# A graph network on one core: no scratch writes between the gathers, attention fetched two chunks ahead, products copied out by ScalarE

## The chip, the cores and the metric

The kernel runs on one core of a Trainium2 chip. The metric is the device time of one execution in microseconds (us). Five engines work side by side, each through its own queue of instructions: TensorE (PE; its weight loads are listed as PEld), VectorE (DVE), ScalarE (ACT), GpSimd (POOL) and SyncE (SP, which here only issues transfers). SBUF is the on-chip memory of 128 partitions, PSUM the small memory that TensorE writes its products to.

## The reference, cut to what matters

There are 6250 nodes with 128 features and 200,000 edges, sorted by destination `dst`; `src` is random. Two convolutions over edges are followed by one attention over edges. All is float32.

```python
def mesh_conv(x, src, dst, ea, w1, b1, g, bt, w2, b2):
    m = jnp.concatenate([x[dst], x[src], ea], axis=-1) @ w1 + b1
    m = jax.nn.silu(group_norm(m, g, bt))
    m = m @ w2 + b2
    out = jax.ops.segment_sum(m, dst, num_segments=n)
    return out / jnp.clip(cnt, 1.0)[:, None]

h = mesh_conv(x, ...);  h = silu(group_norm(h));  h = h + time_embedding
h = mesh_conv(h, ...);  h = silu(group_norm(h)) + x
q, k, v = (h @ w + b).reshape(n, 8, 16)            # three products
logits = (q[dst] * k[src]).sum(-1) * scale + (edge_attr @ ew + eb)
amax = segment_max(logits, dst)
pe = jnp.exp(logits - amax[dst])
w = pe / jnp.clip(segment_sum(pe, dst)[dst], 1e-06)
o = segment_sum(w[:, :, None] * v[src], dst).reshape(n, D) @ ow + ob
return h + group_norm(o, an_g, an_b)
```

What matters for the change: rows of a table are fetched for every edge by `src` (a gather), rows for `dst` come from a product with a one-hot matrix, and the two are added (convolutions) or multiplied (attention).

## The kernel before

**Stages.** After a preparation there are three edge stages in a row: `conv(1)`, `conv(2)` and attention (`pipeline(3, Stage(bp))`, L1374). Each goes over 196 chunks of 1024 edges (8 tiles of 128). A stage ends with node work for the nodes that are left (`last_nodes`); most nodes are done in batches of four times 128 while the edges run (`conv_nodes`, `attention_nodes`, advanced one piece per step of the pipeline).

**Fetching a chunk** (`fetch` of each `Stage`). `loads` (L598) has SP bring the `pk` rows (the window of 112 destination rows, one of three buffers) and, for every two chunks, `ohT`: the destinations of 2048 edges spread over 112 partitions (896 KB, L592) and their attributes (L595). `gather` (L620) has POOL issue eight indirect transfers (L622), one for each tile of 128 edges, from `b_d` (convolutions, 512 bytes a row) or `kv_d` (attention, keys and values, 1024 bytes a row) into a tile `g`. After the eight it issues `rest` writes of zeros to a scratch tile `nst2` (L634), which nobody reads. `issue_after` keeps their place in POOL's queue: behind the gathers of this chunk and ahead of the next. `REST` (L28) gives 1, 2 and 4 such writes a chunk for the three stages.

**Working on a chunk.** `compared` (L613) has ACT turn `ohT` into a one-hot matrix in two passes (L615, L616). `products` has PE multiply it with `pk` (L1002 in the convolutions, L1181 in attention, there into three PSUM tiles `qe` of at most three tiles of edges each, 136 columns a tile: 128 of q and 8 of the edges' bias). In the convolutions `first` adds the gathered rows (L1008). In attention `first` calls `logits` (L1185): VectorE multiplies `qe` with the gathered keys, once for each `qe` tile (L1190), ACT copies the bias columns to `ebs` (L1191), VectorE sums over each head (L1193) and adds the bias (L1195).

**Attention, later work.** Chunks are taken together in runs of up to eight. `maxima` is a generator that finds the running maxima of a run: transposes on PE, scans on VectorE (L1222, L1225), a subtraction (L1233), the exponent on ACT (L1235) and eight small products (L1237). `second` advances it between the instructions of the chunk that it works on: a one-hot (L639), `add_late` (L1273 to L1279), `weighted` (ACT copies into `v` at L1246, VectorE's product with the gathered values at L1247), the sums by destination on PE (L1254), and `merge_late` (L1287 to L1269). Chunk n-9 is worked on in step n. The pool `gp` holds 11 tiles `g`, `vp` one tile `v`.

**Order.** `pipeline` (L713) writes out the order by hand: a step n fetches chunk n + `ahead`, and so on down the list. `in_order` (L701) then fixes that order on VectorE, SP, ACT and PE, each for itself; POOL is not in that list. With `ahead = 2` (convolutions) the products of chunk n+1 come right after the fetch, with `ahead = 1` (attention) at the end of the step. Waits between engines are added from what the tiles need: a tile in a pool of n buffers waits until the last reader of the n-th tile before it is done.

The heart of the step, and the end of `maxima`'s use in `second`:

```python
        stage.root(run)
        if n + ahead < NCH:
            compared(ks[n + ahead])
        stage.second(run, [ks.pop(c) for c in seconds])
        if n < NCH:
            stage.first(ks[n])
```

Of the kernel before, what the change touches and what calls it, by code (L numbers as in the profile page):

```python
# [8 lines left out]
FP = mybir.dt.float32  # L9
BF = mybir.dt.bfloat16  # L10
I32 = mybir.dt.int32
AF = mybir.ActivationFunctionType
ALU = mybir.AluOpType
AX = mybir.AxisListType
# [7 lines left out]
P = 128  # L22
D = 128
H = 8
HD = 16
NT = 8
CH = NT * P
REST = {1: 1, 2: 2, 3: 4}  # L28
G = 8
GC = 2  # L30
BN = 4
# [4 lines left out]
DB = D + H  # L36
# [9 lines left out]
def kernel(ctx: ExitStack, tc: tile.TileContext, x, src, dst, eat, w, out):  # L46
# [9 lines left out]
    nc = tc.nc  # L56
    N = x.shape[0]
    EW = src.shape[1]
    NCH = EW // NT
# [5 lines left out]
    const = ctx.enter_context(tc.tile_pool(name="const", bufs=1))  # L65
# [7 lines left out]
    hpc = gpc.enter_context(tc.tile_pool(name="hpc", bufs=1))  # L73
# [5 lines left out]

    ident = const.tile([P, P], FP, name="ident")  # L80
    make_identity(nc, ident)
    iota_i = const.tile([P, P], I32, name="iota_i")
    nc.gpsimd.iota(iota_i, pattern=[[1, P]], base=0, channel_multiplier=0)
    iota_pi = const.tile([P, 1], I32, name="iota_pi")
    nc.gpsimd.iota(iota_pi, pattern=[[1, 1]], base=0, channel_multiplier=1)
# [234 lines left out]
    for t in pk:  # L320
        nc.vector.memset(t, 0.0)

    temb = const.tile([P, D], FP, name="temb")
    squares = {n: const.tile([P, D], FP, name=f"w_{n}") for n in ("c1_w2", "c2_w2", "ow")}
    qkv_t = const.tile([P, 3, D], FP, name="qkv_t")

# [386 lines left out]
    def pipeline(i, stage, aside=iter(())):  # L713

        start = len(nc.cur_bb.bb.instructions)  # L720
        ends, todo = steps_of(i)
        starts = {n: j for j, (n, _) in enumerate(plans[i])}
        ahead = stage.ahead
        ks, under_way = {}, []
        for c in range(ahead):
            ks[c] = stage.fetch(c)
            compared(ks[c])
        stage.products(ks[0])
        for n, seconds in enumerate(todo):
            if n + ahead < NCH:  # L730
                ks[n + ahead] = stage.fetch(n + ahead)
            if n + 1 < NCH and ahead == 2:
                stage.products(ks[n + 1])
            run = [ks[c] for c in ends.get(n, ())]
            stage.root(run)
            if n + ahead < NCH:
                compared(ks[n + ahead])
            stage.second(run, [ks.pop(c) for c in seconds])
            if n < NCH:
                stage.first(ks[n])  # L740
            if n + 1 < len(todo) and todo[n + 1]:
                stage.early(ks[todo[n + 1][0]])
            if n in starts:
                for _ in aside:
                    pass
                under_way.append(stage.batch(starts[n]))
            for g in list(under_way):
                if next(g, STOP) is STOP:
                    under_way.remove(g)
            if n > 4:  # L750
                next(aside, None)
            if n < NCH:
                stage.reduce(ks[n])
            if n + 1 < NCH and ahead == 1:
                stage.products(ks[n + 1])
        stage.flush()
        for g in (*under_way, aside):
            for _ in g:
                pass
        in_order(start)  # L760
# [205 lines left out]
    def conv(i):  # L966
# [4 lines left out]
        with ExitStack() as es:  # L971
            pool = lambda n, b, **kw: es.enter_context(tc.tile_pool(name=f"{n}{i}", bufs=b, **kw))
# [72 lines left out]
            class Stage:  # L1045
# [4 lines left out]
                def fetch(self, c):  # L1050
# [3 lines left out]
                    k.h = hs[c % len(hs)]  # L1054
                    return k

                def products(self, k):
                    hidden(k, [(k.ohT[:KW], k.pk[:KW, :D])])

# [103 lines left out]
    with ExitStack() as es:  # L1163
        pool = lambda n, b, **kw: es.enter_context(tc.tile_pool(name=f"{n}a", bufs=b, **kw))
        pools = {"oh": pool("oh", 2), "ps": pool("ps", 1, space=PSUM)}
        gp, wk, vp = pool("gp", G + 3), pool("wk", 2), pool("vp", 1)
        ps_ = pools["ps"]
        iota = ps_.tile([P, D], FP, name="iota")
        nc.vector.tensor_copy(iota, iota_j)
# [3 lines left out]

        def products(k, terms):

            for a in range(0, NT, TB):
                qe = ps_.tile([P, TB, DB], FP, name="qe", tag="qe", bufs=3)
                for t in range(min(TB, NT - a)):
                    e = slice((a + t) * P, (a + t + 1) * P)
                    for j, (lhs, rhs) in enumerate(terms):  # L1180
                        nc.tensor.matmul(qe[:, t, :], lhsT=lhs[:, e], rhs=rhs,  # L1181
                                         start=(j == 0), stop=(j == len(terms) - 1))
                k.qe.append(qe)

        def logits(k, lg):  # L1185
            ebs = wk.tile([P, NT, H], FP, name="ebs")
            for a, qe in zip(range(0, NT, TB), k.qe):
                n = min(TB, NT - a)
                kk = k.g[:, a:a + n, :D]
                nc.vector.tensor_tensor(kk, qe[:, :n, :D], kk, ALU.mult)  # L1190
                nc.scalar.copy(ebs[:, a:a + n, :], qe[:, :n, D:])  # L1191
            l3 = wk.tile([P, NT, H], FP, name="l3")
            nc.vector.tensor_reduce(  # L1193
                l3, k.g[:, :, :D].rearrange("p t (h c) -> p t h c", c=HD), AX.X, ALU.add)
            nc.vector.tensor_tensor(lg, l3, ebs, ALU.add)  # L1195

        def load_runs(run, bp):

# [97 lines left out]
            add(k, t3[:, bass.ds(k.win, 2), :], 2)  # L1296

        class Stage:
            ahead = 1
            sums, late, nb = [], [], None  # L1300
            lg, j = None, 0

# [5 lines left out]
            def fetch(self, c):  # L1308
                k = loads(c, pools, a_d[3], self.ahead)
                k.g = gp.tile([P, NT, KV], FP, name="g")  # L1310
                gather(k, k.g, kv_d, REST[3])
                k.qe = []
                return k

            def products(self, k):
                products(k, [(k.ohT[:KW], k.pk[:KW])])

            def first(self, k):
                if self.j == 0:
# [14 lines left out]
            def second(self, run, ks):  # L1334


                pieces = iter(())
                if run:
                    pieces = maxima(run, self.lg, self.nb, self.bp)
                    self.nb, self.j = None, 0  # L1340
                for n, k in enumerate(ks):
                    mine = pieces if n == len(ks) - 1 else iter(())
                    next(mine, None)
                    onehot(k, pools, iota)
                    next(mine, None)


                    if self.late:
                        add_late(self.late.pop(0))
                    next(mine, None)  # L1350
                    weighted(k)
                    nc.scalar.copy(k.v[:, :, VK:VK + H], k.wl)
                    nc.scalar.copy(k.v[:, :, VK + H], ef[:, k.c * NT:(k.c + 1) * NT])
                    sums(k, VK + H + 1)
                    if self.sums:
                        merge_late(self.sums[0])
                        self.late.append(self.sums.pop())
                    self.sums.append(k)
                for _ in pieces:
                    pass  # L1360

            def batch(self, j):
# [17 lines left out]
        def left(k):  # L1380
            lp = pools["left"]
            left_rows(k, pools, a_d[3], "qe", [P, TB, DB], 3)
            k.g = gp.tile([P, NT, KV], FP, name="g")
            gather(k, k.g, kv_d)
            k.qe = []
            products(k, [(k.ohf.rearrange("p t e -> p (t e)"), k.rows), (k.ea, webl)])
            lg = lp.tile([P, NT, H], FP, name="l_lg")
            logits(k, lg)
            neg = lp.tile([P, 4, P], FP, name="l_neg")
            part = lp.tile([P, H, 2], FP, name="l_part")  # L1390
            junk = lp.tile([P, 4, P], FP, name="l_junk")
            for a in range(2):
                nc.vector.tensor_scalar(neg, k.ohf[:, 4 * a:4 * a + 4, :], 1.0, BIG, ALU.subtract, ALU.mult)
                for h in range(H):
                    bc = ps_.tile([P, 4, P], FP, name="l_bc", tag="blk")
                    for t in range(4):
                        nc.tensor.transpose(bc[:, t, :], lg[:, 4 * a + t, h:h + 1].to_broadcast([P, P]), ident)
                    nc.vector.tensor_tensor_reduce(
                        junk, bc, neg, 1.0, -BIG, ALU.add, ALU.max, part[:, h, a:a + 1])
            cm = lp.tile([P, H], FP, name="l_cm")  # L1400
            nc.vector.tensor_reduce(cm, part, AX.X, ALU.max)
            me = ps_.tile([P, NT, H], FP, name="l_me", tag="pe")
            for t in range(NT):
                nc.tensor.matmul(me[:, t, :], lhsT=k.ohf[:, t, :], rhs=cm, start=True, stop=True)
            nc.vector.tensor_tensor(lg, lg, me, ALU.subtract)

            nc.vector.tensor_scalar(lg, lg, 0.0, None, ALU.min)
            k.pe = lp.tile([P, NT, H], FP, name="l_pe")
            nc.scalar.activation(k.pe, lg, AF.Exp)
            weighted(k)  # L1410
            sums(k, VK)
            tt = t3[:, bass.ds(k.win, 1), :]
            merge(k, M[:, bass.ds(k.win, 1), :], None, cm[:, None, :], 1)
            add(k, tt, 1)
# [43 lines left out]
```

## Time and profile before

| | |
|---|---|
| time, median of 3 runs | 6840.58 us (6835.94 to 6841.69) |
| the profiled execution | 6827.89 us |
| span of its profile, first to last instruction | 6826.1 us |
| busy PE / DVE / ACT / POOL | 3811.6 (56%) / 5134.4 (75%) / 3310.5 (48%) / 5154.2 (76%) us |
| granted clock of TensorE, mean | 0.736 |
| gathers, L622 | 4704, mean 959 ns (convolutions) and 980 ns (attention) |
| scratch writes, L634 | 1372, mean 432 ns, 593.2 us busy |
| transfers | 800.41 MB, mean 117 GB/s |

How to read it: a line of a group names the line of the kernel, engine, operation, output and inputs (sizes as partitions x elements), the count, then the busy time and the mean duration of one in ns, then the engine's idle time just before them and what ended it. In a view by time the first two numbers are the start and the duration in us. A wait is put down to the event that came last. Matmul times are modelled, and POOL's spans are rough.

### The profile page before, as it was taken

How to read it: one execution, taken by the hardware profiler on the slowest of the kernel's cores; microseconds unless marked ns; L12 is line 12 of the kernel's file. 1: busy time of each engine (PE TensorE's matmuls, PEld its weight loads, DVE VectorE, ACT ScalarE, POOL GpSimd, SP SyncE). 2: the span in 40 equal slices, each digit the busy share in tenths (PEclk: the TensorE clock that was granted, in tenths of full speed). 3: DMA queues.
4: the chain of work that ended last, by engine and by line, in shares of the span. 5: the costliest groups of instructions: out<-in, count | busy, mean ns of one | idle time of the engine just before them, and what ended most of it. 6: DMA issues, size and time to landing. Idle time of an engine off the chain costs nothing. (4 is left out here: it accounts for less than half of the span.)

```text
span 6826.1 us, 73476 instructions
## 1 busy us (share of the span) xinstructions
PE 3811.6 (56%) x20957; PEld 3602.1 (53%) x20958; DVE 5134.4 (75%) x7564; ACT 3310.5 (48%) x5293; POOL 5154.2 (76%) x6090
## 2 busy tenths in 40 slices
PE   5555555555554555555555555455555555555555
PEld 4555555555554555555555555445545555555554
DVE  7877888888886777777777777556677777777777
ACT  5666566666665555555555555322233333333332
POOL 5777777777775777777777777577777777777774
PEclk8777777777777767677777777677777777777777
DMA  5544444444443433334444344354555555555543
GB/s 155 127 109 103 101 118 107 113 109 108 108 112 82 99 98 96 96 98 104 111 104 109 104 108 110 100 136 134 136 142 138 143 143 143 138 141 144 143 135 84
DMA packets 414317, 800.41 MB, mean 117 GB/s; under 512 B 101813, under 2 KB 274984, under 8 KB 379496
## 3 DMA queue, kind: packets, MB, share of 16 engines
q0 software_dynamic: 175616, 411.34, 24.3%
q1 hardware_dynamic: 232646, 380.69, 19.9%
q10 hardware_dynamic: 5632, 3.51, 0.2%
q8 instruction: 172, 2.82, 0.2%
q14 instruction: 251, 2.06, 0.1%
HBM read 754.19 MB, written 40.96 MB: 116 GB/s over the span
## 5 line engine op out<-in xcount | busy, mean ns | idle before, releaser
L622 POOL DMA_INDIRECT g<-b_d,src_i x3136 | 3006.1, 959 | 951.9 <-issue 913.6
L1032 PE MATMUL u<-h,oh 128*128 128x129 f32 (+1 forms) x6272 | 1276.9, 386 | 1474.2 <-ACT h L1027 1473.9
L1032 PEld LDWEIGHTS u<-h,oh 128*128 128x128 f32 x6272 | 1178.6, 289 | 1557.0 <-ACT h L1027 1553.3
L622 POOL DMA_INDIRECT g<-kv_d,src_i x1568 | 1536.8, 980 | 500.8 <-issue 470.4
L1002 PE MATMUL m<-pk,ohT 117*128 117x128 f32 x6272 | 1005.3, 328 | 340.9 <-DVE h L1008 298.2
L1254 PE MATMUL u<-v,oh 128*128 128x145 f32 x3136 | 760.1, 430 | 764.7 <-DVE nm L1287 763.0
L1002 PEld LDWEIGHTS m<-pk,ohT 117*128 117x128 f32 x6272 | 965.9, 243 | 368.9 <-DVE h L1008 320.1
L1254 PEld LDWEIGHTS u<-v,oh 128*128 128x128 f32 x3136 | 707.0, 312 | 799.7 <-issue 799.7
L1008 DVE TENSOR_TENSOR h<-m,g 128x1024 f32<-128x1024 f32 x392 | 478.7, 1221 | 817.8 <-DMA g<-b_d,src_i 800.9
L1010 ACT ACTIVATE sq<-h 128x1024 f32<-128x1024 f32 x392 | 414.3, 1057 | 817.6 <-DVE h L1008 817.0
L1027 ACT ACTIVATE h<-h 128x1024 f32<-128x1024 f32 x392 | 414.3, 1057 | 653.8 <-DVE h L1026 637.2
L1190 DVE TENSOR_TENSOR g<-qe,g 128x384 f32<-128x384 f32 (+1 forms) x588 | 294.6, 511 | 549.0 <-DMA g<-kv_d,src_i 512.0
L615 ACT ACTIVATE ohT<-ohT,minus_p 112x1024 f32<-112x1024 f32 x588 | 670.5, 1140 | 16.4 <-DMA ohT<-rel_d 16.2
L616 ACT ACTIVATE ohT<-ohT 112x1024 f32<-112x1024 f32 x588 | 621.5, 1057 | 18.6
L634 POOL MEMSET nst<- 128x392 f32 x1372 | 593.2, 432 | 45.4
L1181 PE MATMUL qe<-pk,ohT 117*128 117x136 f32 x3136 | 514.9, 320 | 152.2 <-ACT ebs L1191 146.1
L1181 PEld LDWEIGHTS qe<-pk,ohT 117*128 117x128 f32 x3136 | 477.2, 227 | 186.5 <-ACT ebs L1191 180.2
L1011 DVE TENSOR_REDUCE var<-sq 128x64 f32<-128x1024 f32 x392 | 476.4, 1215 | 41.0 <-ACT sq L1010 40.4
L1025 DVE TENSOR_TENSOR h<-h,cps 128x1024 f32<-128x1024 f32 x392 | 478.5, 1221 | 13.4
L1026 DVE TENSOR_TENSOR h<-h,cps 128x1024 f32<-128x1024 f32 x392 | 478.4, 1220 | 13.4
L1191 ACT COPY ebs<-qe 128x24 f32<-128x24 f32 (+1 forms) x588 | 104.1, 177 | 769.7 <-DVE g L1190 769.2
L639 DVE TENSOR_TENSOR oh<-cps,dm 128x1024 f32<-128x1024 f32 x392 | 476.1, 1215 | 0.2
(265 smaller groups left out, 4736.4 us busy)
## 6 DMA issues: line engine op xcount, KB each, us to landing
ohT<-rel_d SPq DMA_DIRECT2D x294, 896.0 KB
g<-b_d,src_i POOLq DMA_INDIRECT x3136
pk<-a_d SPq DMA_DIRECT2D x588, 56.0 KB
g<-kv_d,src_i POOLq DMA_INDIRECT x1568
ohT<-in_eat_dram SPq DMA_DIRECT2D x294, 40.0 KB
a_d<-n_o SPq DMA_DIRECT2D x28, 256.0 KB
kv_d<-n_o SPq DMA_DIRECT2D x28, 256.0 KB
n_h<-h_d SPq DMA_DIRECT2D x19, 256.0 KB
```

The costliest lines, as they stand in the source:

```text
L615: nc.scalar.activation(k.ohT[:WN, :], k.ohT[:WN, :], AF.Square, bias=minus_p[:WN])
L616: nc.scalar.activation(k.ohT[:WN, :], k.ohT[:WN, :], AF.Relu, bias=1.0, scale=-4.0)
L622: return nc.gpsimd.indirect_dma_start(out=g[:, t, :table_d.shape[1]], out_offset=None, in_=table_d, in_offset=bass.IndirectOffsetOnAxis(ap ...
L634: last = nc.gpsimd.memset(nst2, 0.0)
L1002: nc.tensor.matmul(k.m[:, t, :], lhsT=lhs[:, t * P:(t + 1) * P], rhs=rhs, start=(j == 0), stop=(j == len(terms) - 1))
L1008: nc.vector.tensor_tensor(k.mt, k.m, k.g, ALU.add)
L1011: return lambda: nc.vector.tensor_reduce(var[:, j * NT * H:(j + 1) * NT * H], sq.rearrange("p t (g c) -> p (t g) c", c=HD), AX.X, ALU.add)
L1025: nc.vector.tensor_tensor(k.mt, k.mt, over_edges(gam), ALU.mult)
L1026: nc.vector.tensor_tensor(k.mt, k.mt, over_edges(bet), ALU.add)
L1032: nc.tensor.matmul(k.u[:, :wide], lhsT=k.oh[:, t, :], rhs=k.h[:, t, :wide], start=(t == 0), stop=(t == NT - 1))
L1181: nc.tensor.matmul(qe[:, t, :], lhsT=lhs[:, e], rhs=rhs, start=(j == 0), stop=(j == len(terms) - 1))
L1254: nc.tensor.matmul(k.u[:, :wide], lhsT=k.oh[:, t, :], rhs=k.v[:, t, :wide], start=(t == 0), stop=(t == NT - 1))
```

## The change

It does three things.

1. `REST` becomes 0 for every stage: POOL issues no scratch write, and its queue holds gathers only while edges run.
2. Attention goes from `ahead = 1` to `ahead = 2`: chunk n+2 is fetched in step n, and the products of chunk n+1 are issued right after that fetch.
3. A new step `evicted` has ACT copy whole products, q and bias, from the three `qe` tiles in PSUM to one tile `k.q` in SBUF (pool `qp`, one buffer, 8 x 136 elements a partition). VectorE's product is then one instruction of 128x1024 elements, with both inputs in SBUF. `evicted` of chunk n+1 comes after `first` of chunk n and after `finish`, which now runs what is left of `maxima` (before, `second` did so ahead of `first`). In the convolutions `evicted` and `finish` do nothing.

Two small tiles, `iota_i` and `temb`, move to the pool `hpc`, which is given back before attention.

```diff
-REST = {1: 1, 2: 2, 3: 4}
+REST = {1: 0, 2: 0, 3: 0}
...
-    iota_i = const.tile([P, P], I32, name="iota_i")
+    iota_i = hpc.tile([P, P], I32, name="iota_i")
...
-    temb = const.tile([P, D], FP, name="temb")
+    temb = hpc.tile([P, D], FP, name="temb")
...
         stage.products(ks[0])
+        stage.evicted(ks[0])
         for n, seconds in enumerate(todo):
             if n + ahead < NCH:
                 ks[n + ahead] = stage.fetch(n + ahead)
-            if n + 1 < NCH and ahead == 2:
+            if n + 1 < NCH:
                 stage.products(ks[n + 1])
...
             if n < NCH:
                 stage.first(ks[n])
+            stage.finish()
+            if n + 1 < NCH:
+                stage.evicted(ks[n + 1])
...
-            if n + 1 < NCH and ahead == 1:
-                stage.products(ks[n + 1])
...
-        gp, wk, vp = pool("gp", G + 3), pool("wk", 2), pool("vp", 1)
+        gp, wk, vp, qp = pool("gp", G + 3), pool("wk", 2), pool("vp", 1), pool("qp", 1)
...
-        def logits(k, lg):
-            ebs = wk.tile([P, NT, H], FP, name="ebs")
+        def evicted(k):
+
+            k.q = qp.tile([P, NT, DB], FP, name="q")
             for a, qe in zip(range(0, NT, TB), k.qe):
                 n = min(TB, NT - a)
-                kk = k.g[:, a:a + n, :D]
-                nc.vector.tensor_tensor(kk, qe[:, :n, :D], kk, ALU.mult)
-                nc.scalar.copy(ebs[:, a:a + n, :], qe[:, :n, D:])
+                nc.scalar.copy(k.q[:, a:a + n, :], qe[:, :n, :])
+
+        def logits(k, lg):
+            kk = k.g[:, :, :D]
+            nc.vector.tensor_tensor(kk, k.q[:, :, :D], kk, ALU.mult)
             l3 = wk.tile([P, NT, H], FP, name="l3")
             nc.vector.tensor_reduce(
-                l3, k.g[:, :, :D].rearrange("p t (h c) -> p t h c", c=HD), AX.X, ALU.add)
-            nc.vector.tensor_tensor(lg, l3, ebs, ALU.add)
+                l3, kk.rearrange("p t (h c) -> p t h c", c=HD), AX.X, ALU.add)
+            nc.vector.tensor_tensor(lg, l3, k.q[:, :, D:], ALU.add)
...
         class Stage:
-            ahead = 1
+            ahead = 2
...
-                for _ in pieces:
+                self.pieces = pieces
+
+            def finish(self):
+                for _ in self.pieces:
                     pass
```

More of the change, by code (lines that the diff above doesn't have):

```diff
@@ L1055, in fetch, with evicted @@
                     return k
+                def evicted(self, k):
+                    pass
+                def finish(self):
+                    pass
                 def products(self, k):
@@ L1174, in products @@
         def products(k, terms):
+            k.qe = []
             for a in range(0, NT, TB):
@@ L1311, in fetch @@
                 gather(k, k.g, kv_d, REST[3])
-                k.qe = []
                 return k
@@ L1316, in products, with evicted @@
                 products(k, [(k.ohT[:KW], k.pk[:KW])])
+            def evicted(self, k):
+                evicted(k)
             def first(self, k):
@@ L1358, in second, with finish @@
                     self.sums.append(k)
-                for _ in pieces:
+                self.pieces = pieces
+            def finish(self):
+                for _ in self.pieces:
                     pass
@@ L1384, in left @@
             gather(k, k.g, kv_d)
-            k.qe = []
             products(k, [(k.ohf.rearrange("p t e -> p (t e)"), k.rows), (k.ea, webl)])
+            evicted(k)
             lg = lp.tile([P, NT, H], FP, name="l_lg")
```

## The prediction

> **What bounds the kernel now.** First view: the busy time of each engine in a quiet stretch of each edge stage (columns: length; busy PE, PEld, DVE, ACT, POOL; granted clock; DMA share; GB/s), then the gathers of L622 in each stage.
>
> ```profile
> 1200.00:1800.00 600.00, 344.88 (x2055) 330.30 (x2053) 494.20 (x542) 378.04 (x475) 467.30 (x521) 0.76 0.43 109
> 2400.00:2900.00 500.00, 282.84 (x1465) 266.68 (x1464) 362.80 (x343) 281.48 (x341) 384.36 (x455) 0.71 0.38 96
> 5200.00:6400.00 1200.00, 679.44 (x3498) 636.62 (x3498) 880.05 (x1952) 380.91 (x1057) 939.63 (x1182) 0.72 0.52 141
> ...
> L622 POOL DMA_INDIRECT g<-b_d,src_i x1568: 940/944/2628, 55.9 to 2097.2; - x196
> L622 POOL DMA_INDIRECT g<-b_d,src_i x1568: 938/944/1442, 2148.9 to 4311.8; - x196
> L622 POOL DMA_INDIRECT g<-kv_d,src_i x1568: 942/946/2938, 4368.2 to 6753.0; - x196
> ```
>
> POOL reads as 78% busy, but L622 is preceded each time by 0.30 us that nothing explains ("issue"), so POOL is in fact always occupied. From first to last gather the stages take 2041.3, 2162.9 and 2384.8 us, by 195.9 chunks of eight 10.42, 11.04 and 12.17 us a chunk. Next, POOL in order of time at a chunk's end, one pair from each stage.
>
> ```profile
> 1018.79 0.45 POOL L634 MEMSET nst<- 128x392 f32 x1
> 1019.41 0.95 POOL L622 DMA_INDIRECT g<-b_d,src_i  x1 [0.16 <-issue]
> ...
> 3012.90 0.93 POOL L634 MEMSET nst<- 128x392 f32 x2
> 3014.13 0.95 POOL L622 DMA_INDIRECT g<-b_d,src_i  x1 [0.30 <-issue]
> ...
> 5408.14 1.89 POOL L634 MEMSET nst<- 128x392 f32 x4
> 5410.34 0.95 POOL L622 DMA_INDIRECT g<-kv_d,src_i  x1 [0.31 <-issue]
> ```
>
> Gathers start every 1.25 us (5411.59, 5412.85, ...), eight take 9.99. The undisturbed chunk is 10.29 (1019.41 to the next first gather at 1029.70), 10.96 or 10.9 (3014.13 to 3025.09) and 11.89 us (5410.34 to 5422.23). So the scratch writes cost 0.30, 0.92 and 1.89 us a chunk. The waits say who stands behind POOL:
>
> ```profile
> DVE h L1008 <- DMA g<-b_d,src_i: 142.9, 41, 6.4
> DVE g L1190 <- DMA g<-kv_d,src_i: 226.5, 161, 4.7
> POOL g L622 <- DMA g<-b_d,src_i: 12.5, 41, 0.3
> ```
>
> VectorE waits for gathered rows (the first line from 3300 to 4000 us, the second from 5200 to 6400); the same view for 1200 to 1800 us gives 82.1 us. POOL waits for nobody longer than 0.6 us inside a stage. The gathers' issue is the bound of all three stages.
>
> **The change, part by part.** (1) *Scratch writes in the two convolution stages.* 195 x 0.30 = 58 and 195 x 0.92 = 179 us, if others keep up. VectorE is busy 494/600 x 10.42 = 8.6 and 363/500 x 11.04 = 8.0 us a chunk (up to 8.9 where node batches run), below 9.99; its waits other than for gathers were 15 us in 600. ACT is at 6.6. I take 237 us; lower bound 190, if a fifth of it is lost to uneven steps; no gain above 237 from here.
>
> (2) *Scratch writes in attention*: 195 x 1.89 = 368 us if POOL stayed the only bound and its gathers as quick. Neither holds, by (3) and (4).
>
> (3) *The logit product now reads SBUF twice.* L1190 read PSUM and SBUF in three pieces; the new one reads k.q and k.g, both in SBUF, 128x1024 at once. What a two-SBUF-input instruction does to a gather, the scan L1225 shows:
>
> ```profile
> 4854.90 2.28 DVE L1225 TENSOR_TENSOR_SCAN fw<-nbe,fw 64x1024 f32<-64x1024 bf16 x1
> 4855.05 2.89 POOL L622 DMA_INDIRECT g<-kv_d,src_i  x1 [0.30 <-issue]
> ...
> L797 DVE TENSOR_TENSOR n_A<-n_A,r_an_g 128x512 f32<-128x512 f32 x12 | 8.3, 692 | 0.4
> L1247 DVE TENSOR_TENSOR v<-g,pe 128x1024 f32<-128x1024 f32 x98 | 118.8, 1212 | 0.0
> L778 ACT COPY n_x<-nd 128x512 f32<-128x512 f32 x13 | 7.7, 591 | 0.6 <-PE nd L776 0.4
> ```
>
> The gather that starts under the scan ends 0.76 us after it (2.89 us for 0.95); gathers that had already begun are not lengthened, nor is L797 (both inputs in SBUF). The new product lasts about 1.22 us (L1247's size), some 0.31 less than the three pieces (0.56 + 0.56 + 0.42). Nearly each one catches a gather's start (1.22 of 1.25), and holds it 0 to 1.2 us, on average 0.6. If VectorE starts right as the last gather lands, 2.8 us after its start (5419.10 to 5421.93), the phase is fixed: product from 2.85 to 4.07, gather starts at 2.50 and 3.75, held 0.2. I take 0.4; ends 0.2 and 0.7. POOL's chunk: 9.99 + 0.28 (today's excess, 12.17 - 11.89) + 0.4 = 10.67.
>
> The Trainium skill (SBUF — State Buffer, Who interferes with whom) says that a two-SBUF-input VectorE instruction and a GpSimd one that reads SBUF exclude each other for their whole length, by who came first. The stretched gather agrees; L797's unchanged 692 ns does not show the other half. By that half the sum would be the third rival's.
>
> (4) *ScalarE copies all products.* Three copies of 408, 408 and 272 elements replace three of 24, 24 and 16 (179, 179, 173 ns). By L778 (591 ns for 512 elements) and these, 0.83 us per thousand: 0.50 + 0.50 + 0.39 = 1.39, about 1.5 with starts, 0.9 us more a chunk. ACT was busy 381/1200, so load is no matter; order is. qp has one buffer, so the copies of chunk n+1 wait for L1195 of chunk n, the last reader. Queued behind them on ACT are L615 and L616 (1.15 + 1.06) and L1246, for which L1247 on VectorE waits:
>
> ```profile
> 5423.64 1.06 ACT L616 ACTIVATE ohT<-ohT 112x1024 f32<-112x1024 f32 x1
> 5424.60 0.26 ACT L1246 COPY v<-pe 128x64 f32<-128x64 f32 x1
> 5426.49 1.22 DVE L1247 TENSOR_TENSOR v<-g,pe 128x1024 f32<-128x1024 f32 x1
> ```
>
> Today L1246 is 1.6 us early here. After: from the end of L1195 ACT needs 1.5 + 2.24 + 0.26 = 4.1 us with gaps; VectorE comes to L1247 after 2.7 (5423.85 to 5426.49). So L1247 slips 1.4 us. A step of VectorE is then 4.1 + 2.43 (L1247 to the next L1190, 5414.63 to 5417.06) + 2.8 (new product, L1193, L1195) = 9.3 us. Every eighth step also runs the maxima (scans 1.21 + 1.27 + 2.28, L1233 0.68, L1237 8 x 0.21 overlapped to 1.13: 6.6), where the slip is hidden: 9.3 - 1.4 + 6.6 less the overlap of starts, about 14; the step after it loses some 1.2, as ACT's exponent (0.60) and L1233 come first. Without nodes eight steps are 6 x 9.3 + 14 + 10.5 = 80.3, 10.0 a chunk. The 19 node batches (from chunk 44 on) add some 8.8 us of VectorE each, of which steps with slip hide half, and on ACT 0.59 + 0.63 + 0.32 + a table load of 1.28: 86 us, 10.7 a chunk.
>
> (5) *Two chunks ahead, other order.* Products of n+1 are issued a step earlier, so PE's waits on the qe copies (31 us in 1200) and L1190's waits on PE (18 us) go. SP issues the same DMAs, pk one step earlier, the ohT pair (bound today by PE's release of the old pair, 796 us of SP waiting) about as now; with a full step of lead I cost them at nothing. If that lead fails, L615 waits and the 4.1 us of ACT grow by the lateness. gp still has 11 buffers: gather n+2 needs L1247 of n-9, two steps before its use (some 19 us against 10 + 2.8), no wait. `finish` after the logits moves work without adding any. Moving iota_i and temb to another pool, and the path for left-over edges, which has no instruction in the trace: nothing.
>
> **Sum.** POOL's 10.67 and VectorE's 10.0 to 10.7 lie close, and where two loops lie close each pays some of the other's unevenness: I take 10.85. Attention gains 195 x (12.17 - 10.85) = 257 us. In all 237 + 257 = 494 from the profiled execution's 6827.9 (span 6826.1): 6334. The median of the runs is 12.7 us above that execution, so 6346.
>
> **Rivals.** *Only POOL counts* in attention, phase fixed: 9.99 + 0.28 + 0.2 = 10.47, gain 332, in all 569: 6272. For it: VectorE alone has 1.3 us less work than POOL today; against: the slip through L1246. *The ACT chain decides*: if also L615 waits on ohT or the copies on PE, 11.5 a chunk: gain 131 and 190 to 237 before: 6473 to 6520. *Whole-instruction exclusion*: the product waits for the running gather (up to 0.95) and then holds POOL for 1.22 less the 0.30 of issue, 0.92 each: 9.99 + 0.28 + 0.92 = 11.2; gain 189, in all 426: 6415. *Slower*: each gather also waits for an earlier one's landing (third wait line, 41 times, at most 0.3 us), so if rows landed late, POOL would stand in every stage. Before, a landing took 2.8 us, up to VectorE's waits of 6.4 when the big ohT load runs. It costs from about eight gathers, 10 us, and decides against the change above the mean chunk of 11.2 us; at 11.5 in all stages 588 x 0.3 = +176: 7017. Against it: DMA share 0.52, which at 10.85 instead of 12.17 is only 0.58. *The scratch writes were no cost*: POOL would fill the room by waiting elsewhere, 6841; the pairs above speak against it.
>
> **Chances.** Forecast 0.60 (own range 6260 to 6440), only POOL 0.12, ACT chain 0.13, exclusion 0.06, slower 0.07, no change 0.02. Faster 0.91, same 0.02, slower 0.07; "same" is within 0.2%, what a measurement of this kernel can tell. The range 6240 to 6525 takes in the first four and the ends of (1), (3) and (4).
>
> **What would show it.** No L634 on POOL; a chunk of 10.1 us in both convolutions, L1008 still waiting for g; in attention gathers lengthened once a chunk under the new product, its duration near 1.22, and L1247 waiting some 1.4 us on L1246. A gather that waits on a landing for whole us, or one lengthened outside two-SBUF work, would prove me wrong; so would a chunk above 11.5 in attention.

## The result, and the profile after

The changed kernel takes 6311.62 us (6307.04 to 6316.12, four runs) beside 6841.14 us of the kernel before (6835.94 to 6843.72, four runs). The ratio is 0.9227, with a 95% interval of 0.9211 to 0.9243. Profiled execution against profiled execution it is 6316.12 against 6827.89 us, 511.8 us less; the span is 6314.1 us.

Busy time in a quiet stretch of each stage comes first, with the same columns as before, and below it the source view of L622 (count, then shortest, median and longest in ns, then first and last start).

```profile
1200.00:1800.00 600.00, 348.77 (x2145) 336.31 (x2146) 507.34 (x557) 391.50 (x492) 455.19 (x476) 0.79 0.44 113
2400.00:2900.00 500.00, 278.81 (x1605) 263.97 (x1605) 396.18 (x376) 308.70 (x376) 378.38 (x399) 0.78 0.41 107
4600.00:6000.00 1400.00, 887.06 (x4672) 816.47 (x4672) 1146.66 (x2345) 591.88 (x1414) 1078.66 (x1055) 0.74 0.60 162
```

```profile
L622 POOL DMA_INDIRECT g<-b_d,src_i x3136: 940/947/2629, 55.9 to 4075.8; - x196
L622 POOL DMA_INDIRECT g<-kv_d,src_i x1568: 942/949/2894, 4134.9 to 6203.8; - x196
```

POOL is busy for about the same share as before (0.76 to 0.77 in the three stretches), yet every one of its instructions there is now a gather. With the 0.30 us of issue ahead of each one the engine is still never free. From first to last gather the stages take 1988.8, 1975.5 and 2068.9 us (the first convolution ends at 2044.7, the second begins at 2100.3). The differences to before are 52.5, 187.4 and 315.9 us. The gaps between stages grew by 6.7 us, and the time from the last gather's start to the end of the span by 37.2 (from 73.12 to 110.35). 52.5 + 187.4 + 315.9 - 6.7 - 37.2 = 511.9, the whole difference but for rounding.

Next, the waits: first VectorE's longest from 200 to 2000 us, in the first convolution, where it still waits for gathered rows (L1010 is the old L1008); then those from 4600 to 6000 us, in attention (engine, line, what it waited for; us in total, times, longest).

```profile
DVE h L1010 <- DMA g<-b_d,src_i: 224.2, 85, 6.3
...
ACT q L1199 <- DVE lg L1207: 329.6, 112, 7.4
POOL g L622 <- issue: 306.7, 1006, 0.3
...
PE qe L1190 <- ACT q L1199: 184.5, 114, 6.1
DVE v L1259 <- ACT v L1258: 80.3, 51, 2.8
...
DVE fw L1234 <- PE lt L1231: 47.4, 16, 3.2
...
DVE g L1203 <- DMA g<-kv_d,src_i: 17.5, 64, 4.8
...
POOL g L622 <- DMA g<-kv_d,src_i: 4.0, 13, 0.3
```

Before, VectorE stood 226.5 us in 1200 of attention for gathered rows. Now that is 17.5 in 1400, and two other waits of VectorE have come up: for ScalarE's copies into `v` (L1258 is the old L1246), and for the transposes `lt` of the maxima on PE. POOL still waits for nobody longer than 0.3 us. The same stretch in order of time shows where both engines lose time (start, duration, engine, line; idle time before in brackets):

```profile
5002.30 0.95 POOL L622 DMA_INDIRECT g<-kv_d,src_i  x1 [0.30 <-issue]
...
5002.64 1.22 DVE L1203 TENSOR_TENSOR g<-q,g 128x1024 f32<-128x1024 f32 x1
5003.56 1.12 POOL L622 DMA_INDIRECT g<-kv_d,src_i  x1 [0.30 <-issue]
...
5005.15 0.22 DVE L1207 TENSOR_TENSOR lg<-l,q 128x64 f32<-128x64 f32 x1
...
5005.46 1.19 ACT L1199 COPY q<-qe 128x408 f32<-128x408 f32 x3 [2.88 <-DVE lg L1207]
...
5008.19 1.13 ACT L615 ACTIVATE ohT<-ohT,minus_p 112x1024 f32<-112x1024 f32 x1
...
5009.36 1.06 ACT L616 ACTIVATE ohT<-ohT 112x1024 f32<-112x1024 f32 x1
...
5010.32 0.25 ACT L1258 COPY v<-pe 128x64 f32<-128x64 f32 x1
...
5010.61 1.22 DVE L1259 TENSOR_TENSOR v<-g,pe 128x1024 f32<-128x1024 f32 x1 [2.53 <-ACT v L1258]
...
5013.31 1.23 DVE L1203 TENSOR_TENSOR g<-q,g 128x1024 f32<-128x1024 f32 x1 [0.20 <-issue]
...
5013.74 1.61 POOL L622 DMA_INDIRECT g<-kv_d,src_i  x1 [0.30 <-issue]
```

L1207 is the last reader of `q`, and from its end runs the chain that the prediction described: three copies, L615, L616, L1258, and only then L1259. Here a node batch adds 1.6 us on ScalarE (a table load and L921, 5006.67 to 5008.29), and L1259 starts 2.53 us late. The gather at 5013.74 begins 0.43 us into the new product and takes 1.61 us instead of 0.95: it ends 0.81 us after the product.

### The profile page after: what moved, and what is told of

It reads as the page before. It is cut to its first block, busy times and chain, and to the rows that moved or that the text cites. A ratio compares the mean times of both kernels' runs of the same rounds, so it can differ in the third digit from the quotient of the medians.

```text
span 6314.1 us, 71784 instructions
## 1 busy us (share of the span) xinstructions
PE 3687.3 (58%) x20957; PEld 3471.6 (55%) x20958; DVE 5088.1 (81%) x7172; ACT 3432.3 (54%) x5293; POOL 4622.8 (73%) x4718
## 5 line engine op out<-in xcount | busy, mean ns | idle before, releaser
L622 POOL DMA_INDIRECT g<-b_d,src_i x3136 | 3010.7, 960 | 971.4 <-issue 855.4
L622 POOL DMA_INDIRECT g<-kv_d,src_i x1568 | 1591.7, 1015 | 499.2 <-issue 454.2
L1004 PE MATMUL m<-pk,ohT 117*128 117x128 f32 x6272 | 938.3, 313 | 228.1 <-DVE h L1010 187.7
L1004 PEld LDWEIGHTS m<-pk,ohT 117*128 117x128 f32 x6272 | 903.9, 229 | 249.7 <-DVE h L1010 203.2
L1010 DVE TENSOR_TENSOR h<-m,g 128x1024 f32<-128x1024 f32 x392 | 477.7, 1219 | 571.9 <-DMA g<-b_d,src_i 568.1
L1266 PE MATMUL u<-v,oh 128*128 128x145 f32 x3136 | 641.8, 379 | 334.1 <-DVE nm L1299 332.9
L1266 PEld LDWEIGHTS u<-v,oh 128*128 128x128 f32 x3136 | 594.1, 267 | 376.1 <-issue 376.1
L1190 PE MATMUL qe<-pk,ohT 117*128 117x136 f32 x3136 | 591.4, 362 | 336.5 <-ACT q L1199 331.6
L1190 PEld LDWEIGHTS qe<-pk,ohT 117*128 117x128 f32 x3136 | 543.3, 260 | 384.6 <-ACT q L1199 378.6
L615 ACT ACTIVATE ohT<-ohT,minus_p 112x1024 f32<-112x1024 f32 x588 | 673.8, 1146 | 20.3 <-DMA ohT<-rel_d 20.3
L616 ACT ACTIVATE ohT<-ohT 112x1024 f32<-112x1024 f32 x588 | 621.2, 1057 | 18.5
L1199 ACT COPY q<-qe 128x408 f32<-128x408 f32 (+1 forms) x588 | 233.0, 468 | 554.3 <-DVE lg L1207 531.3
L1027 DVE TENSOR_TENSOR h<-h,cps 128x1024 f32<-128x1024 f32 x392 | 478.5, 1221 | 13.5
L1028 DVE TENSOR_TENSOR h<-h,cps 128x1024 f32<-128x1024 f32 x392 | 478.4, 1220 | 13.4
L639 DVE TENSOR_TENSOR oh<-cps,dm 128x1024 f32<-128x1024 f32 x392 | 475.6, 1213 | 0.2
L1024 DVE TENSOR_TENSOR h<-h,cps 128x1024 f32<-128x1024 f32 x392 | 475.2, 1212 | 0.0
L1279 ACT ACTIVATE u<-d 128x16 f32<-128x16 f32 x196 | 36.7, 187 | 612.4 <-DVE d L1275 609.8
```

The lines of the kernel that those rows point to most:

```text
L615: nc.scalar.activation(k.ohT[:WN, :], k.ohT[:WN, :], AF.Square, bias=minus_p[:WN])
L616: nc.scalar.activation(k.ohT[:WN, :], k.ohT[:WN, :], AF.Relu, bias=1.0, scale=-4.0)
L622: return nc.gpsimd.indirect_dma_start(out=g[:, t, :table_d.shape[1]], out_offset=None, in_=table_d, in_offset=bass.IndirectOffsetOnAxis(ap ...
L639: return nc.vector.tensor_tensor(k.oh, iota[:, None, :].to_broadcast([P, NT, P]), k.dm[:, :, None].to_broadcast([P, NT, P]), ALU.is_equal)
L1004: nc.tensor.matmul(k.m[:, t, :], lhsT=lhs[:, t * P:(t + 1) * P], rhs=rhs, start=(j == 0), stop=(j == len(terms) - 1))
L1010: nc.vector.tensor_tensor(k.mt, k.m, k.g, ALU.add)
```

## The experiments

Nearly every reading rests on one account. In attention POOL's time from first to last gather is 1567 steps of the undisturbed 1.251 to 1.254 us, 1960 to 1965 us, plus what gathers last beyond their usual 0.945 us ("held"), plus scratch writes where there are any (1.89 us a chunk before, 0.30 in `e4_one_write_in_new_attention`). In every row of the table that sum comes within some 3 us of the first column. "Tail" is from the last gather to the end of the span. All four columns are worked out from the traces.

| kernel | first to last gather | held | of it under the logit product | tail |
|---|---|---|---|---|
| before | 2384.8 | 53.2 | 0 | 73.1 |
| changed | 2068.9 | 106.6 | 66.7 | 110.4 |
| `e1_no_writes_old_attention` | 2002.9 | 43.9 | 0 | 101.0 |
| `e3_two_q_tiles` | 2080.7 | 119.5 | 74.5 | 98.8 |
| `e4_one_write_in_new_attention` | 2129.4 | 108.7 | 57.4 | 104.3 |
| `e9_onehot_from_sbuf_again` | 2067.4 | 108.6 | 0 | 93.0 |
| `e10_two_q_tiles_three_pieces_again` | 2045.2 | 83.2 | 34.4 | 95.5 |
| `e11_three_pieces_alone_again` | 2028.9 | 65.5 | 22.2 | 111.6 |
| `e12_no_writes_scan_in_halves` | 1985.4 | 26.7 | 0 | 100.9 |

Runs ran in groups on different chips, so times are compared by their ratios to the kernel before beside them.

### The writes alone

`e1_no_writes_old_attention` is the kernel before with only the writes gone; `e2_no_writes_convolutions_only` keeps those of attention.

```diff
-REST = {1: 1, 2: 2, 3: 4}
+REST = {1: 0, 2: 0, 3: 0}      # e1
+REST = {1: 0, 2: 0, 3: 4}      # e2
```

> Kernel before with REST = 0 in all stages and nothing else: attention keeps ahead = 1 and reads its products from PSUM. Theory (the rest of the change is not needed, VectorE's loop of the old attention is only 8.2 us, 10.0 with node batches): attention becomes bound by POOL at 9.99 + 0.28 = 10.3 us a chunk, gathers are lengthened only by scans and node work (excess near the 53 us of before, not 107), total 6841 - 52 - 187 - 195 x 1.88 = 6235 us (6210 to 6270), below the changed kernel's 6312. Rival (the new attention is what lets VectorE use the time that POOL gains; with products only at the end of a step VectorE waits on PE): attention above 11.3 us a chunk, 6440 us or more.

> Kernel before with REST 0, 0, 4: the writes go in the two convolutions alone. Theory (stages are independent, POOL bounds both): first gather to last 1989 and 1976 us as in the changed kernel, attention 12.17 us a chunk as before, total 6841 - 52 - 187 = 6602 us (6590 to 6615). Rival (the gain of the convolutions hangs together with the rest of the change, or part of it comes from elsewhere): off by over 30 us.

`e1_no_writes_old_attention`: 6240.31 us (6236.65 to 6243.59), ratio 0.9128 (0.9112 to 0.9143). `e2_no_writes_convolutions_only`: 6595.05 us (6588.37 to 6597.53), ratio 0.9643 (0.9627 to 0.9659). Both came out as the theory said. The convolutions' writes cost 6832.79 - 6595.05 = 238 us; those of attention 0.9643 - 0.9128 = 0.0515 of 6841, 352 us. And the rest of the change, the rebuilt attention, loses: 0.9227 - 0.9128 = 0.0099, 68 us. In the traces the two attention stages differ by 66.0 us (2068.9 - 2002.9), and the held time by 62.7 (106.6 - 43.9). What the fetch two chunks ahead is worth by itself no run shows. The waits of `e1_no_writes_old_attention` from 4600 to 6000 us:

```profile
DVE g L1190 <- DMA g<-kv_d,src_i: 76.4, 37, 5.2
...
DVE v L1247 <- ACT v L1246: 4.8, 6, 1.4
```

With the old order VectorE loses 4.8 us to ScalarE's copies where the changed kernel loses 80.3, and it waits for gathers: POOL is its bound, at 10.23 us a chunk.

### Does VectorE's loop through ScalarE decide?

After the result my view was that VectorE's step, lengthened by the slip of L1259, sets the pace of the changed attention, with POOL just behind. `e3_two_q_tiles` takes the slip away by a second `q` tile (room for it comes from rows that only the convolutions use, moved to `hpc`). `e4_one_write_in_new_attention` instead puts one scratch write a chunk back into attention.

```diff
-        rows[name] = const.tile([P, D], FP, name=f"r_{name}")
+        rows[name] = (const if name in ("ob", "an_g", "an_b") else hpc).tile([P, D], FP, name=f"r_{name}")     # e3
...
-        gp, wk, vp, qp = pool("gp", G + 3), pool("wk", 2), pool("vp", 1), pool("qp", 1)
+        gp, wk, vp, qp = pool("gp", G + 3), pool("wk", 2), pool("vp", 1), pool("qp", 2)     # e3
...
-REST = {1: 0, 2: 0, 3: 0}
+REST = {1: 0, 2: 0, 3: 1}      # e4
```

> Changed kernel with two buffers for k.q (to make room, rows that only the convolutions use are held in the pool that is given back before attention). The copies of chunk n+1 no longer wait for L1207 of chunk n, so the slip at L1259 should go. Theory (VectorE's loop through ACT bounds the changed attention, POOL stands close behind): L1259's wait on L1258 falls from 0.6 us a chunk to under 0.2, VectorE waits for gathers again, attention falls to POOL's 10.4 to 10.55, and the end no longer trails the last gather: 6312 - 40 to 70 = 6240 to 6275 us. Rival (POOL's own 10.57 us a chunk is the bound already): 6305 to 6315 us.

> Changed kernel with one scratch write a chunk in attention (REST 0, 0, 1), which makes POOL 0.30 us a chunk slower. Theory (VectorE's 10.7 us a step is the bound, POOL has 0.15 us to spare and is some chunks ahead at the end): +0 to +35 us, 6312 to 6347. Rival (POOL is the bound): +58 us, 6370.

`e3_two_q_tiles`: 6313.4 us (6306.53 to 6316.55), ratio 0.9231 (0.9216 to 0.9247), the same as the changed kernel. Its waits on VectorE from 4600 to 6000 us:

```profile
DVE g L1203 <- DMA g<-kv_d,src_i: 128.8, 86, 7.3
...
DVE v L1259 <- ACT v L1258: 15.8, 17, 1.3
DVE fw L1234 <- PE lt L1231: 8.9, 10, 1.6
```

The slip fell from 80.3 to 15.8 us and the wait for `lt` from 47.4 to 8.9, as meant; the 103 us saved went whole into waiting for gathers, which rose from 17.5 to 128.8. (PE's wait for ScalarE's copies, L1190, fell from 184.5 to 27.2 us.) `e4_one_write_in_new_attention`: 6364.5 us (6355.54 to 6371.28), ratio 0.9307 (0.9291 to 0.9322), so 0.008 of 6841 = 55 us more than the changed kernel. That is nearly a whole write a chunk (195 x 0.30 = 58) and not the 0 to 35 of an engine with slack. The theory failed in both.

### What holds the gathers?

If POOL is the bound, its held gathers are the price. Three edits change what holds them. `e9_onehot_from_sbuf_again` takes `e1_no_writes_old_attention` and lets the one-hot L639, a product of the same size, read its `iota` from SBUF instead of PSUM, so that both its inputs lie in SBUF. `e11_three_pieces_alone_again` cuts the changed kernel's logit product into three instructions; `e10_two_q_tiles_three_pieces_again` does that on top of `e3_two_q_tiles`.

```diff
-        iota = ps_.tile([P, D], FP, name="iota")
-        nc.vector.tensor_copy(iota, iota_j)
+        iota = iota_j                                                       # e9
...
-            nc.vector.tensor_tensor(kk, k.q[:, :, :D], kk, ALU.mult)
+            for a in range(0, NT, TB):                                      # e10, e11
+                b = min(a + TB, NT)
+                nc.vector.tensor_tensor(kk[:, a:b], k.q[:, a:b, :D], kk[:, a:b], ALU.mult)
```

These kernels first ran as `e5_old_attention_onehot_from_sbuf`, `e6_two_q_tiles_three_pieces` and `e7_three_pieces_alone`, all in one group on one chip:

> The first run's kernel (no scratch writes, old attention) with one operand moved: the one-hot L639 of attention reads its row of numbers from SBUF in place of PSUM, so that one instruction of 128x1024 a chunk has two SBUF inputs, as the changed kernel's product has; nothing else differs. Theory (such an instruction holds the gather that starts under it): L639 keeps its 1.22 us, some 160 to 190 gathers are lengthened under it, by 60 to 110 us in all, attention goes from 10.23 to 10.5 or 10.75 us a chunk, total 6240 + 55 to 100 = 6295 to 6340 us. Rival (the 72 us between the first run and the changed kernel come from the order, the copies or the fetch two ahead, not from the port): 6235 to 6250 us.

> The third run's kernel (changed kernel with two q tiles) with the logit product cut into three instructions of 3, 3 and 2 tiles, still from SBUF. A shorter instruction catches a gather's start more rarely and holds it less: by width squared over twice the 1.25 us, 0.32 us a chunk in place of 0.60, so the product's share of the lengthening should fall from 74.5 us to some 40. VectorE pays 0.3 us a chunk more, of which it has 0.9 to spare there. Theory (POOL with its held gathers is the bound once VectorE's slip is gone): 6313 - 25 to 45 = 6270 to 6290 us. Rival (something else keeps that kernel at 6313, VectorE included): 6310 to 6370 us.

> The changed kernel with the product in three pieces and still one q tile. POOL gains some 0.15 us a chunk as in the run beside it, but VectorE's loop through ACT, 10.7 us a step, grows by 0.3. Theory (two loops of nearly the same length, either one holds the time): no gain, 6312 + 0 to 60 us; VectorE stops waiting for gathers altogether and falls further behind them. Rival (POOL alone is the bound of the changed attention): 6270 to 6290 us, as with two q tiles.

They took 7930.13, 7915.77 and 7927.58 us, and the kernel before beside them 7474.23 (7458.76 to 7490.78) instead of 6833. The ratios are 1.0613 (1.0589 to 1.0637), 1.0598 (1.0569 to 1.0628) and 1.0605 (1.0584 to 1.0627). Three kernels that differ by up to 27 us elsewhere lie within 15 us here, so these runs tell nothing of what holds the gathers; what they show is taken up at the end. The same three kernels again on another two chips:

> The fifth run's kernel (no scratch writes, old attention, L639 reading SBUF twice), repeated since TensorE's stops covered what it was to show. Where the kernel before takes 6840 us: theory (held gathers) 6295 to 6340, rival (order and copies) 6235 to 6250. Where it takes 7470: 7930 again.

> The sixth run's kernel (two q tiles, product in three pieces), repeated for the same reason. Where the kernel before takes 6840 us: theory 6270 to 6290, rival 6310 to 6370. Where it takes 7470: 7915 again.

> The seventh run's kernel (changed kernel, product in three pieces, one q tile), repeated since TensorE's stops covered what it was to show. Where the kernel before takes 6840 us: theory (POOL with its held gathers and VectorE's loop through ACT are nearly of one length, so relief of one alone gains little): POOL's hold under the product falls from 67 us to some 35, but VectorE's steps do not fall below today's 10.7 us and it waits even less for gathers: 6305 to 6365 us. Rival (POOL alone is the bound of the changed attention): 6270 to 6290 us, as with two q tiles.

And the changed kernel beside the first two of them, as a control:

> The changed kernel once more, beside the same kernel before as the two repeats below. Theory A (the change is worth the same on every chip): ratio 0.92 again, 6312 us if the kernel before takes 6840. Theory B (the second set of runs was on a chip where TensorE is stopped for 1 to 3 us at a time and the kernel before takes 7474; there the faster pace costs more than it gains): if the kernel before takes some 7470 us here, the changed kernel takes 7900 to 7950; if it takes 6840, 6312.

`e8_changed_again`: 6304.83 us (6300.02 to 6311.53), ratio 0.9234 (0.9219 to 0.925), as at first. `e9_onehot_from_sbuf_again`: 6295.18 us (6286.32 to 6300.19), ratio 0.9219 (0.9204 to 0.9235). That is 55 us more than without the edit (62 by the ratios), from the place of one operand, at the lower end of what its theory had. The stage is 64.5 us longer than there, and the held time 64.7. In its trace L639 now stretches 127 gathers by 67.2 us; in `e1_no_writes_old_attention` it stretched none. In order of time:

```profile
5016.40 1.22 DVE L639 TENSOR_TENSOR oh<-iota_j,dm 128x1024 f32<-128x1024 f32 x1
5016.88 1.56 POOL L622 DMA_INDIRECT g<-kv_d,src_i  x1 [0.30 <-issue]
5018.74 0.95 POOL L622 DMA_INDIRECT g<-kv_d,src_i  x1 [0.30 <-issue]
```

The gather starts 0.48 us into L639 and ends 0.82 us after it, just as under the changed kernel's product. So here it is the second input in SBUF that holds it, with nothing else of the new attention in the kernel.

`e10_two_q_tiles_three_pieces_again`: 6272.09 us (6270.68 to 6276.97), ratio 0.9184 (0.9169 to 0.9199), and `e11_three_pieces_alone_again`: 6267.99 us (6265.14 to 6275.03), ratio 0.918 (0.9166 to 0.9194). Cutting the product is worth 0.0047 of 6841 = 32 us with two `q` tiles and as much with one (0.9227 - 0.918). The first came out as its theory said. In the second the theory of two loops of nearly one length failed again: the time is that of its rival, POOL alone, even 2 us below it. The trace of `e11_three_pieces_alone_again`:

```profile
5018.58 1.37 DVE L1205 TENSOR_TENSOR g<-q,g 128x384 f32<-128x384 f32 x3
5019.02 0.95 POOL L622 DMA_INDIRECT g<-kv_d,src_i  x1 [0.30 <-issue]
5020.27 0.94 POOL L622 DMA_INDIRECT g<-kv_d,src_i  x1 [0.30 <-DVE g L1205]
```

A gather that starts 0.44 us into the product, nearly the phase of the one above that took 1.61 us, is no longer stretched: the piece that it starts under lasts only 0.55 us, and the next two don't hold it. Under the product gathers are held 22.2 us instead of 66.7, and the stage is 40 us shorter. VectorE's waits of the same kernel from 4600 to 6000 us:

```profile
DVE v L1261 <- ACT v L1260: 82.2, 51, 2.8
...
DVE fw L1236 <- PE lt L1233: 36.4, 17, 3.2
...
DVE g L1205 <- DMA g<-kv_d,src_i: 4.3, 2, 4.1
```

The slip is all there (82.2 against 80.3 us), and the product in pieces is longer (2 x 0.554 + 0.416 = 1.52 us against 1.225), yet VectorE's step fell from 10.69 to 10.45 us (mean over chunks 50 to 185). POOL's own step there went from 10.64 to 10.39. So VectorE's loop could go at 10.45 or less, and 10.69 was POOL's pace. Whether it could go much below 10.45 these runs don't show, as it hardly waits for gathers there.

### A version that beats both

The largest hold left in `e1_no_writes_old_attention` is that of the backward scan L1225, which has two inputs in SBUF: 31.9 us on 24 gathers. `e12_no_writes_scan_in_halves` takes that kernel and cuts the scan into two instructions, the second going on from the first one's end.

```diff
-            nc.vector.tensor_tensor_scan(
-                fw[:q, ::-1], nb["nbe"][:q, ::-1], fw[:q, ::-1], -BIG, ALU.add, ALU.max)
+            for at, start in ((slice(CH - 1, half - 1, -1), -BIG), (slice(half - 1, None, -1), fw[:q, half:half + 1])):
+                nc.vector.tensor_tensor_scan(
+                    fw[:q, at], nb["nbe"][:q, at], fw[:q, at], start, ALU.add, ALU.max)
```

> The first run's kernel (no scratch writes, old attention) with the backward scan L1225, the one long instruction there that reads SBUF twice, cut into two halves of 512. POOL's held gathers are 44 us there, 32 of them under this scan (1.3 us a time). Theory: two halves of some 1.2 us hold a gather for some 0.6 to 0.9 us in all, the sum falls to 15 to 22 us, total 6240 - 5 to 15 = 6225 to 6235 us where the kernel before takes 6835 (ratio 0.911 to 0.912), if VectorE's additional 0.1 us every eighth step does not count. Rival (VectorE's step with the maxima decides there): 6240 to 6250 us.

It takes 6215.47 us (6214.37 to 6221.38), ratio 0.9104 (0.9091 to 0.9116), the fastest of all. By the ratios that is 16 us less than `e1_no_writes_old_attention` (the two intervals just overlap), where its theory had 5 to 15. In order of time:

```profile
4865.96 2.53 DVE L1226 TENSOR_TENSOR_SCAN fw<-nbe,fw 64x512 f32<-64x512 bf16 x2
4866.50 1.43 POOL L622 DMA_INDIRECT g<-kv_d,src_i  x1 [0.30 <-issue]
4868.23 1.01 POOL L622 DMA_INDIRECT g<-kv_d,src_i  x1 [0.30 <-issue]
```

The two halves take 2.53 us instead of 2.28, but the gather under them is 1.43 us where it was 2.89 before. The scan's hold fell from 31.9 to 10.6 us, all holds from 43.9 to 26.7, and the stage from 2002.9 to 1985.4: 17.5 us. The other 8 us of the difference lie ahead of attention, where the two kernels are the same (first gather at 4126.3 against 4134.2), so they are not the scan's.

## Why the prediction was right, and where it was not

The time came within its own range (6346 forecast, 6311.62 measured), and the mechanism held in the main: POOL's gathers stayed the bound and the new product holds them. That the total came so close is in part luck. Against the profiled execution the sum stood at 6334, and 6316.1 was measured, 18 us less: attention gained 59 us more than forecast (315.9 against 257) and the convolutions 3 more, while the tail and the gaps between stages, which the sum left out, cost 44. The rest of the difference comes from the 12.7 us added for the median, which this time lies 4.5 below the profiled execution. Point by point:

**The writes on POOL.** Right in mechanism and size: 58 and 179 us forecast, 52.5 and 187.4 measured, and 238 by `e2_no_writes_convolutions_only` against 237. In attention the bound of 368 us "if POOL stayed the only bound" stands against 352 in `e1_no_writes_old_attention`, where the old order was kept.

**The product that reads SBUF twice.** Right: 0.4 us a chunk taken, 66.7/196 = 0.34 measured, on 185 gathers; duration 1.225 us where 1.22 was forecast. By the Trainium skill (SBUF — State Buffer, Who interferes with whom) a VectorE instruction with two SBUF inputs contends with a GpSimd instruction that reads SBUF. `e9_onehot_from_sbuf_again` agrees, if a gather counts as such an instruction: 67.2 us from one operand's place. The other half of that rule, that a GpSimd instruction which came first blocks VectorE for its whole length, is not borne out: 170 of the 196 products started while a gather was running, as at 5002.64, and those lasted 1225 ns on average, the other 26 1227 ns. That was the third rival.

**The slip of L1259.** Right as a mechanism and in the size of one slip, but too frequent in the sum: it came 51 times in 131 chunks, 80.3/51 = 1.57 us each, where 1.4 us was forecast for seven steps of eight without node work; the three copies take 1.19 us where 1.5 was allowed. Two more things were wrong about it. The step that cost the earlier products at nothing, and expected PE's waits for the copies (31 us in 1200) to go, missed that PE's queue now stands behind ScalarE's copies of `q` (L1190, 184.5 us in 1400 above): the `lt` transposes come late, 47.4 us in 131 chunks. And neither wait cost the stage anything: `e3_two_q_tiles` took away 103 us of both and the time stayed.

**The sum's failed step** is "where two loops lie close each pays some of the other's unevenness: I take 10.85". Measured are 10.56 us a chunk (2068.9/195.9), which is POOL alone: (1965 + 106.6)/196 = 10.57. The 10.85 was not worked out from anything, and VectorE's 10.7 beside it was itself set a little high: 80.3/8 and 86 us over the 152 chunks from 44 on make 10.6. Inside the stage the rival *Only POOL counts* was the right reading, with the hold at 0.34 instead of its 0.2; `e3_two_q_tiles`, `e4_one_write_in_new_attention` and `e11_three_pieces_alone_again` each say so. The mistake was some 195 x 0.28 = 55 us.

**A missing term made up for most of it**: the tail, 37.2 us longer. The source view of the backward scan from 5800 us on shows why (the counts after each size):

```profile
L1237 DVE TENSOR_TENSOR_SCAN fw<-nbe,fw x7: 2279/2282/2282, 5841.3 to 6266.8; 64x1024 f32<-64x1024 bf16 x4, 48x1024 f32<-48x1024 bf16 x1, 32x1024 f32<-32x1024 bf16 x1, 16x1024 f32<-16x1024 bf16 x1
```

The last runs have 6, 4 and 2 chunks instead of 8 (48, 32 and 16 partitions), and a scan over fewer partitions takes the same 2.28 us. So over the last 12 chunks VectorE needs 13.7 us a step, against POOL's 10.5: 12 x 3.2 = 39 us that it falls behind. Before, its 12.9 lay close to POOL's 12.4 and hardly showed. The mean over the stage hid a part of it where VectorE is the bound. In `e1_no_writes_old_attention` it is 12.7 there, against POOL's 10.3, and the tail 101.0. No run changed the tail by itself, so this account of it is reckoned and not tested.

**The other rivals.** ScalarE's chain as the bound and no change are out by the time. For *Slower* no late landings were seen: POOL's waits for a landing in the stretch above are at most 0.3 us each (the last wait line), and the DMA share is 0.60 (0.58 was reckoned). But a case that no rival named exists, as the last section shows.

## What to carry to other kernels

Where one engine's queue issues all gathers and is never free, every instruction in that queue costs time (0.30 to 0.47 us for each write here), and what others do to the gathers' duration is the next price; the check is whether undisturbed steps plus held time add up to the stage. Beside such a queue VectorE's operands are better left in PSUM, or a two-SBUF-input instruction cut into pieces. After a bound is taken away, look at the stage's end by itself: work whose cost goes by the run and not by the chunk weighs most where runs are short.

## What the runs showed of the hardware that was not expected

In attention a gather is clearly stretched only if it starts under an instruction with two inputs in SBUF, and then ends 0.75 to 0.84 us after it; one that had begun 0.34 us earlier (5002.30, with a product from 5002.64) keeps its 0.95. A held gather thus still needs most of its usual 0.95 us once the product has ended.

Two inputs are not the only cause. In the preparations that run beside the first convolution of the changed kernel, three instructions with one input in SBUF (L531, L567, L571) each held a gather too, by 1.7 us in all:

```profile
845.86 0.97 DVE L567 TENSOR_SCALAR f<-f 128x1568 f32<-128x1568 f32 x1
845.98 1.66 POOL L622 DMA_INDIRECT g<-b_d,src_i  x1 [0.30 <-issue]
```

This gather ends 0.81 us after L567. The prediction named a gather lengthened outside two-SBUF work as a sign against it; for the time, 1.7 us do not count, but its rule was too narrow.

The larger surprise is the chip on which all three kernels without writes were 6% slower than the kernel before, itself 9% slower than elsewhere. `e6_two_q_tiles_three_pieces` and `e10_two_q_tiles_three_pieces_again` are the same kernel. PE in the second convolution, first on that chip, then on another:

```profile
3023.54 0.37 PE L1004 MATMUL m<-pk,ohT 117*128 117x128 f32 x1 [2.43 <-issue]
3027.04 0.37 PE L1004 MATMUL m<-pk,ohT 117*128 117x128 f32 x1 [3.13 <-issue]
3029.20 0.37 PE L1004 MATMUL m<-pk,ohT 117*128 117x128 f32 x1 [1.79 <-issue]
```

```profile
3022.74 0.83 PE L1004 MATMUL m<-pk,ohT 117*128 117x128 f32 x6
```

Matmuls of one group stand 2 to 3 us apart with nothing that the profile shows to wait for, where elsewhere six take 0.83 us. Counted over the trace, there are 793 gaps of more than 0.5 us inside groups (1676 us in sum, an upper estimate, as some records of matmuls are missing) against 51 (134 us). Of these, 712 (1348 us) follow nothing that the profile shows, against 2 (13 us); the kernel took 1644 us longer. The mean granted clock is 0.688 against 0.768, and POOL waits whole microseconds for VectorE, which it doesn't elsewhere; from 5600 to 7000 us:

```profile
POOL g L622 <- DVE cm L1304: 382.5, 55, 13.0
```

So there the gathers stand still behind VectorE. That PE's halts are what holds VectorE up is likely by these counts, but no run shows it by itself. Why PE halts, and why the kernel before, with its writes, was hurt less, stays open: of the kernel before there are only times on that chip (mean clock about 0.705), and the changed kernel was not run on it. That the writes' slower pace helps PE there is a guess that no run tested.
